# Hybrid network on one core: the first image's front and the mask's sorting issued in turns, scans started from their first 128 channels

## Chip, cores and metric

One core of a Trainium2 chip runs the whole program. The metric is the time of one execution on the device in microseconds (us). Its engines are called PE (TensorE, matrix multiplies), DVE (VectorE), ACT (ScalarE), POOL (GpSimd) and SP (SyncE, which here only issues DMAs).

## What is computed

The input is four images of 32 x 32 positions and 256 channels, so 1024 tokens per image. Cut to what matters here:

```python
# layer 0: state-space layer with a convolution
x = layernorm(src); x = x @ w_in + b_in                # 256 -> 512 channels
x = gelu(depthwise_conv3x3(x))                         # "front"
dt = softplus(proj_dt(x)); Bm, Cm = proj_bc(x)         # 64 states
h = exp(dt * A) * h + (dt * x) * Bm;  y = (h * Cm).sum(state)   # scan over 1024 tokens
out = src + layernorm(y + x * D_skip) @ w_out
# layer 1: grouped 3x3 convolution block
# layer 2: attention under a mask, then a mixture of 8 experts
mask = zeros(1024, 1024).at[edges[0], edges[1]].set(True)       # from a list of 69632 edges
# layer 3: state-space layer with 16 states, then a mixture of 8 experts
```

Each scan is linear in the tokens and independent for each pair of channel and state, so 512 channels x 64 states (layer 0) or 512 x 16 (layer 3) rows are scanned along 1024 tokens.

## The kernel before, in words

**Set-up.** `load_vectors` and `prepare` load vectors and weights, build the tables for the scans and store some prepared weights in DRAM. They run before everything else, and a scheduler of the framework orders their instructions.

**Stages.** The work of an image is cut into Python generators: `front(b)` (layer 0 up to the scan's operands), `middle(b)` (the end of layer 0, layers 1 and 2, layer 3 up to its scan's operands), `last(b)` (the end of layer 3 and its experts). Each `yield` is a tick. The table `STAGES` gives their order and the scan that each waits for; `advance` issues the next tick of the current stage. At the end of a front stands `steps`: for d in 0 to 3 (a d is 128 channels) and two halves of the tokens it projects dt on PE, takes the softplus on ACT, DVE and POOL, splits dt * x into three bf16 parts, and stores `dt` and `parts` in DRAM. These eight items go through five steps in a software pipeline (`project, add, split, low, store`); when both halves of a d are stored, `("parts", scan, d)` is put into `self.ready`. The last step of the middle stage is the same `steps` for layer 3.

**Scans.** `scans` runs the eight scans of `SCANS` in one chain of units: a unit is 128 rows of (channel, state), that is 64 units for each d of layer 0 and 16 for each d of layer 3, 1280 in all. For a unit, SP loads dt spread over the states (`load`, four units ahead), ACT takes the exponent (`decay`), PE spreads the parts over the states (`first`), DVE multiplies by B and scans, POOL multiplies by C, PE adds up the states (`pair`). `chunk`, called twelve units ahead (`AHEAD`), loads the rows of B and C at the start of a scan and the tile `S` of parts at the start of each d. Before a scan begins, `need` issues ticks of stages until all of that scan's parts are in `self.ready`.

**Who goes when.** In the scanning part the order of the instructions is the order in which Python issues them (`tc.manual_schedule`). Between the units, up to two ticks of stages are issued where a clock kept by `Metered` says that the other engines have time. All of these instructions are recorded with line L120 in the profile.

**The beginning.** `run` issues `front(0)` and `mask_prepare` to the end, outside of the manual order, in pools of their own; the framework's scheduler mixes them. Only then are the pools of the scans opened.

```python
            for _ in self.front(0):
                pass
            self.mask_prepare()
```

**The mask.** `mask_prepare` fills the mask in DRAM (4 MB) with a large negative number, loads the edges, turns them with PE, computes for each edge its place in the mask or none, and sorts the 544 values of each partition on DVE, in 68 rounds of `max` and `match_replace` (L980, L981), so that the edges in use stand in front. The places go to the tile `where` (L986). `scatter` writes zeros to those places, one indirect DMA of 128 words per column of `where`, from POOL's queue; 64 are always issued, later columns only where some partition has so many. One piece of it is issued per unit of the first scan. In the end POOL's queue copies the mask, cast to bf16.

Of the kernel before, what the change touches and what calls it, by code (L numbers as in the profile page):

```python
# [7 lines left out]
F32 = mybir.dt.float32  # L8
# [5 lines left out]
PSUM = bass.MemoryType.PSUM  # L14
DRAM = bass.MemoryType.DRAM

P = 128
# [5 lines left out]
DC = DI // P  # L23
# [7 lines left out]
SCANS = ((0, 0), (0, 1), (3, 0), (0, 2), (3, 1), (0, 3), (3, 2), (3, 3))  # L31

STAGES = (
    ("front", 1, None), ("front", 2, None), ("front", 3, None), ("middle", 0, (0, 0)),
    ("middle", 1, (0, 1)), ("middle", 2, (0, 2)), ("middle", 3, (0, 3)), ("last", 0, (3, 0)),
    ("last", 1, (3, 1)), ("last", 2, (3, 2)),
)
SAFE = 40.0
AHEAD = 12


# [83 lines left out]
class Hybrid:  # L125
# [213 lines left out]
    def scans(self, mp, psum):  # L339
# [7 lines left out]
        nc = self.nc  # L347
# [11 lines left out]
        def chunk(k):  # L359

            if k >= len(units):
                return
            scan, d, c, i, j = units[k]
            if (c, i, j) != (0, 0, 0):
                return
            n = self.states[scan[0]]
            if d == 0:
                self.need(scan)
                bct = self.mem["bc", *scan]
                pair = []  # L370
                for t in range(2):
                    x = mp.tile([P, L], F32, tag=f"rows{t}", name=f"rows{t}", bufs=2)
                    for g in range(P // n):
                        nc.sync.dma_start(x[g * n : (g + 1) * n, :], bct[t * n : (t + 1) * n, :])
                    pair.append(x)
                rows[scan] = pair
            S = mp.tile([3 * 32, 4, L], BF16, tag="S", name="S", bufs=2)
            for s in range(3):
                nc.sync.dma_start(
                    S[32 * s : 32 * s + 32, :, :],  # L380
                    self.mem["parts", *scan, d][s].rearrange("(j p) t -> p j t", p=32),
                )
            chunks[scan, d] = S
# [67 lines left out]

        for k in range(AHEAD):
            chunk(k)
# [5 lines left out]
        for k in range(len(units) + 4):  # L459
# [4 lines left out]
            if k < len(units):  # L464
                a, inp = state.pop(k)
# [9 lines left out]
                pair(k - 2)  # L475
            yield

    def need(self, scan):

        late = False  # L480
        while ("parts", *scan, DC - 1) not in self.ready:
            if self.advance() is None:
                raise RuntimeError(f"{scan} waits for a stage that waits for it")
            late = True
        if late:

            self.clock.update(dict.fromkeys(self.clock, max(self.clock.values())))
# [15 lines left out]
    def run(self):  # L503

        self.done, self.ready = set(), set()
        self.todo, self.stage = list(STAGES), None
        nc, tc = self.nc, self.tc
        with tc.tile_pool(name="fps", bufs=1, space=PSUM) as pp:
            self.side_psum(pp)
            for _ in self.front(0):  # L510
                pass
            self.mask_prepare()
        with tc.tile_pool(name="scan", bufs=1) as mp, tc.tile_pool(
            name="scps", bufs=1, space=PSUM
        ) as psum, tc.tile_pool(name="sdps", bufs=1, space=PSUM) as side, tc.manual_schedule():
            self.side_psum(side)
            scatter = self.scatter()
            clock = self.clock = dict.fromkeys(Metered.COST, 0.0)
            self.nc = Metered(nc, clock)
            for n, _ in enumerate(self.scans(mp, psum)):  # L520
                if n % 2:
                    next(scatter, None)
                now = clock["vector"]
                for e in clock:
                    clock[e] = max(clock[e], now - LAG)
                for _ in range(TICKS):
                    if max(clock.values()) > clock["vector"] + LEAD or self.advance() is None:
                        break
            while self.advance() is not None:
                pass  # L530
            self.nc = nc
        assert not self.todo
        with tc.tile_pool(name="lps", bufs=2, space=PSUM) as pp:
            self.side_psum(pp)
            for _ in self.last(NB - 1):
                pass
# [371 lines left out]
    def mask_prepare(self):  # L908
# [5 lines left out]
        nc, tc = self.nc, self.tc  # L914
# [7 lines left out]
        nc.vector.memset(self.zero, 0.0)  # L922
        self.where = self.const.tile([P, ne], I32, name="where")
        self.more = self.const.tile([1, len(SCATTERS)], I32, name="morei")
        with tc.tile_pool(name="mprep", bufs=1) as mp, tc.tile_pool(
            name="mps", bufs=2, space=PSUM
        ) as pm:
            neg = mp.tile([P, 2048], F32, name="neg")
            nc.gpsimd.memset(neg, NEG)
            flat = self.mask.rearrange("(q p f) o -> q p (f o)", q=4, p=P)  # L930
            for q in range(4):
                nc.sync.dma_start(flat[q], neg)

            ends = mp.tile([P, 2, ne], F32, name="ends")
            for a in range(2):
                raw = mp.tile([P, full + 1, P], I32, tag="raw", name="raw", bufs=2)
                nc.sync.dma_start(
                    raw[:, :full, :],
                    edges[a, : full * P * P].rearrange("(q r p) -> r q p", r=P, p=P),
                )  # L940
                nc.sync.dma_start(
                    raw[:rest, full, :], edges[a, full * P * P :].rearrange("(r p) -> r p", p=P)
                )
                rawf = mp.tile([P, full + 1, P], F32, tag="rawf", name="rawf", bufs=2)
                nc.vector.tensor_copy(rawf[:, :full, :], raw[:, :full, :])
                nc.vector.tensor_copy(rawf[:rest, full, :], raw[:rest, full, :])
                for q in range(full + 1):
                    m = P if q < full else rest
                    ps = pm.tile([P, P], F32, tag="e", name="ps_e")
                    nc.tensor.transpose(ps[:, :m], rawf[:m, q, :], self.ident[:m, :m])  # L950
                    nc.vector.tensor_copy(ends[:, a, q * P : q * P + m], ps[:, :m])
            wrap = mp.tile([P, 2, ne], F32, name="wrap")
            nc.vector.tensor_scalar(wrap, ends, 0.0, float(L), ALU.is_lt, ALU.mult)
            nc.vector.tensor_tensor(ends, ends, wrap, ALU.add)

            ok = mp.tile([P, 2, ne], F32, name="ok")
            nc.vector.tensor_scalar(ok, ends, 0.0, None, ALU.is_ge)
            nc.vector.tensor_scalar(wrap, ends, float(L), None, ALU.is_lt)
            nc.vector.tensor_tensor(ok, ok, wrap, ALU.mult)
            nc.vector.tensor_tensor(ok[:, 0, :], ok[:, 0, :], ok[:, 1, :], ALU.mult)  # L960
            nc.vector.tensor_scalar(ends, ends, 0.0, float(L), ALU.max, ALU.min)

            lin = mp.tile([P, ne], F32, name="lin")
            nc.vector.scalar_tensor_tensor(
                lin, ends[:, 1, :], float(L), ends[:, 0, :], ALU.mult, ALU.add
            )
            nc.vector.scalar_tensor_tensor(lin, lin, 1.0, ok[:, 0, :], ALU.add, ALU.mult)
            cnt = mp.tile([P, 1], F32, name="cnt")
            nc.vector.tensor_reduce(cnt, ok[:, 0, :], AX.X, ALU.add)
            ps = pm.tile([P, P], F32, tag="e", name="ps_c")  # L970
            nc.tensor.transpose(ps[:1, :], cnt, self.ident)
            top = mp.tile([1, 1], F32, name="top")
            nc.vector.tensor_reduce(top, ps[:1, :], AX.X, ALU.max)
            more = mp.tile([1, len(SCATTERS)], F32, name="more")
            for i, (first, _) in enumerate(SCATTERS):
                nc.vector.tensor_scalar(more[:, i : i + 1], top, float(first), None, ALU.is_gt)
            nc.vector.tensor_copy(self.more, more)
            order = mp.tile([P, ne], F32, name="sorted")
            for r in range(0, ne, 8):
                nc.vector.max(out=order[:, r : r + 8], in_=lin)  # L980
                nc.vector.match_replace(  # L981
                    out=lin, in_to_replace=order[:, r : r + 8], in_values=lin, imm_value=0.0
                )
            nc.vector.tensor_scalar(lin, order, 0.0, 2.0 * L * L, ALU.is_le, ALU.mult)
            nc.vector.scalar_tensor_tensor(lin, order, -1.0, lin, ALU.add, ALU.add)
            nc.vector.tensor_copy(self.where, lin)  # L986

    def scatter(self):

# [129 lines left out]
    def shift(self, fp, qT, kT, mT):  # L1119
# [28 lines left out]

        nc.vector.tensor_scalar(most[:, 0:1], most[:, 0:1], SAFE * SAFE, None, ALU.is_lt)
        nc.vector.tensor_scalar(most[:, 0:1], most[:, 0:1], -1.0, 1.0, ALU.mult, ALU.add)  # L1150
# [579 lines left out]
```

## Time and profile before

| | us |
|---|---|
| Median of 3 runs | 7051.57 (7046.13 to 7058.23) |
| Profiled execution, own time | 7061.6 |
| Span of its instructions | 7059.5 |
| Granted PE clock, mean | 0.81 |

| Stretch of the profiled execution | from | to |
|---|---|---|
| Front 0: norm, convolutions, projections | 37.6 | 144 |
| Front 0: `steps`, until its last store is issued | 141 | 209 |
| Rounds of the sort | 171 | 301 |
| Scan (0, 0) | 317.7 | 1386.5 |
| Scans (0, 1), (3, 0), (0, 2), (3, 1), (0, 3) | 1387.8 | 5464.4 |
| Scan (3, 2) | 5465.7 | 6327.7 |
| Scan (3, 3) | 6329.1 | 6643.6 |
| Rest, with `last(3)` | 6643.6 | 7059.5 |

The page of the profile names an engine, a line of the program and an operation as `output<-inputs`. Its slices cut the span in 40 equal parts of 176.5 us; each digit is the share in tenths that an engine was busy. A line of waits gives who waited, for whom, the sum, how often, and the longest, in us. A line of a timeline gives start and duration in us, engine, line, operation, and in brackets how long the engine had been idle and what ended that. An indirect DMA's row on POOL is the time that POOL worked on it, and its landing is a separate number.

### The profile page before, as it was taken

The page shows a single profiled execution, that of the slowest core. Times are in us where ns is not written, and L with a number is a line of the kernel's source. Part 1 is how long each engine was busy: PE and PEld are TensorE (multiplying, and loading weights), DVE is VectorE, ACT ScalarE, POOL GpSimd, SP SyncE. Part 2 cuts the span into 40 slices and gives each one's busy share as a digit, 9 for nine tenths or more (in the row PEclk, how much of TensorE's full clock was granted, in tenths as well). Part 3 has the DMA queues.
Part 4 walks back from the last instruction along what each step waited for, and adds up shares of the span by engine and source line. Part 5 has one row for each costly group of instructions (what it writes and reads, how often), then busy time and mean ns, then how long its engine had stood idle before and what let it go on. Part 6 is the DMA issues. An engine that isn't in the chain of part 4 may idle for free. (4 is left out here: it accounts for less than half of the span.)

```text
span 7059.5 us, 66331 instructions
## 1 busy us (share of the span) xinstructions
PE 5383.6 (76%) x20516; PEld 2218.2 (31%) x20516; DVE 5212.0 (74%) x4477; ACT 3462.1 (49%) x4162; POOL 3650.0 (52%) x1801
## 2 busy tenths in 40 slices
PE   7185876578898567879779668898698677957979
PEld 3020221032253022224235332242254322513556
DVE  2787898887898986789889877898899831247511
ACT  3254666244477324447658434577386332244511
POOL 1288677664556754555766554556656520045300
PEclk9585876578888567979879778898698889877989
DMA  2355666654456565446656654456666620135421
GB/s 82 77 139 158 161 178 167 169 143 120 115 143 176 160 172 136 119 116 171 176 151 164 178 144 120 115 143 178 165 168 165 162 70 6 44 107 152 113 63 33
DMA packets 395053, 939.03 MB, mean 133 GB/s; under 512 B 83268, under 2 KB 165776, under 8 KB 393040
## 3 DMA queue, kind: packets, MB, share of 16 engines
q1 hardware_dynamic: 392512, 932.10, 49.0%
q8 instruction: 172, 2.82, 0.2%
q0 software_dynamic: 2128, 2.13, 0.2%
q14 instruction: 241, 1.97, 0.1%
HBM read 844.17 MB, written 93.95 MB: 133 GB/s over the span
## 5 line engine op out<-in xcount | busy, mean ns | idle before, releaser
L120 POOL TENSOR_TENSOR h<-h,rows 128x1024 f32<-128x1024 f32 x1280 | 3024.2, 2365 | 2138.8 <-DVE h L120 1756.0
L120 DVE TENSOR_TENSOR_SCAN h<-dA,ps_rep 128x1024 f32<-128x1024 f32 x1280 | 2924.7, 2285 | 228.0 <-issue 94.6
L120 DVE TENSOR_TENSOR ps_rep<-ps_rep,rows 128x1024 f32<-128x1024 f32 x1280 | 1553.0, 1213 | 338.7 <-PE ps_rep L120 317.0
L120 ACT ACTIVATE dA<-dA,A_L_conv_A_log 128x1024 f32<-128x1024 f32 x1024 | 1152.8, 1145 | 695.2 <-DMA dA<-dt 600.6
L120 PE MATMUL ps_rep<-S,spread_L_conv_A_log 96*128 96x512 bf16 x2048 | 763.2, 463 | 899.6 <-DVE h L120 731.7
L120 PE MATMUL ps_y<-h,collect_L_conv_A_log 128*32 128x512 f32 x4096 | 750.2, 755 | 91.1 <-POOL h L120 91.1
L120 ACT ACT_TABLE_LOAD x494 | 633.8, 1283 | 174.7 <-DMA dA<-dt 115.0
L120 PEld LDWEIGHTS <-spread_L_conv_A_log 96*128 96x128 bf16 x2048 | 164.5, 103 | 1661.3 <-DVE h L120 1213.5
L120 PE MATMUL ps_h<-xTm,we 128*128 128x512 f32 x1280 | 605.2, 609 | 7.6 <-ACT h_m L120 6.6
L120 PE MATMUL ps_e<-we,h_m 128*128 128x256 f32 x2560 | 587.9, 381 | 10.1 <-ACT h_m L120 10.1
L120 ACT ACTIVATE p<-ps_sc 128x512 f32<-128x512 f32 x512 | 277.9, 595 | 587.2 <-PE ps_sc L120 573.8
L120 ACT ACTIVATE dA<-dA,A_L_attn_A_log 128x1024 f32<-128x1024 f32 x256 | 293.6, 1148 | 490.1 <-DMA dA<-dt 456.4
L120 PEld LDWEIGHTS ps_e<-we,h_m 128*128 128x128 f32 x2560 | 481.8, 190 | 140.6 <-issue 46.0
L120 PE MATMUL ps_at<-p,v 128*32 128x512 f32 x1024 | 363.6, 627 | 63.1 <-ACT p L120 55.7
L120 PE MATMUL ps_rep<-S,spread_L_attn_A_log 96*128 96x512 bf16 x512 | 191.4, 464 | 280.8 <-DVE h L120 239.2
L120 ACT ACTIVATE h_m<-ps_h,cols 128x512 f32<-128x512 f32 x320 | 216.5, 687 | 302.2 <-PE ps_h L120 299.3
L120 DVE SCALAR_TENSOR_TENSOR tb<-ps_e,cw,tb 128x256 f32<-128x256 f32 x448 | 192.6, 473 | 200.5 <-PE ps_e L120 200.5
L120 PEld LDWEIGHTS ps_h<-xTm,we 128*128 128x128 f32 x1280 | 242.4, 193 | 288.1 <-issue 236.3
L120 PE MATMUL ps_sc<-qT,kT 32*128 32x512 f32 x1024 | 300.7, 663 | 0.0
L120 PE MATMUL ps_at<-p,ones 128*32 128x512 f32 x1024 | 280.1, 627 | 0.0
L120 DVE RECIPROCAL sums<-sums 128x512 f32<-128x512 f32 x16 | 53.6, 3353 | 253.4 <-ACT sums L120 253.4
L120 PEld LDWEIGHTS ps_y<-h,collect_L_conv_A_log 128*32 128x32 f32 x4096 | 98.8, 119 | 450.4 <-issue 234.3
(406 smaller groups left out, 5703.5 us busy)
## 6 DMA issues: line engine op xcount, KB each, us to landing
dA<-dt SPq DMA_DIRECT2D x2048, 256.0 KB
dA<-dt SPq DMA_DIRECT2D x2048, 64.0 KB
we<-in_L_ffn_W_dram SPq DMA_DIRECT2D x64, 512.0 KB
parts<-parts SPq DMA_DIRECT2D x64, 384.0 KB
S<-parts SPq DMA_DIRECT2D x96, 256.0 KB
dt<-sp_r SPq DMA_DIRECT2D x64, 256.0 KB
y<-yo SPq DMA_DIRECT2D x128, 128.0 KB
y_back<-y SPq DMA_DIRECT2D x64, 256.0 KB
```

The lines of the kernel that those rows point to most:

```text
L120: return got(*args, **kw)
```

## The change

Front 0 becomes the first entry of `STAGES`, so it is issued by `need` and `advance` in the manual order, like the other fronts. `mask_prepare` becomes a generator, and `scatter` is its end. While `need` issues ticks, it issues two pieces of the mask's work (`SORTS`) after each tick; between the units of the scans one piece follows every unit, as the scatters did before. The first piece loads the edges, six empty pieces follow, then come the turned edges, then the 68 rounds one per piece. The fill of the mask is issued after the edges' loads and turns instead of ahead of the loads. The transposes of the mask take their PSUM tiles from the pool of the stages. `need` asks for the parts of one d instead of all four, and `chunk` calls it for every d. The memory of the sort and that of the scans are then held at the same time.

```diff
 STAGES = (
-    ("front", 1, None), ("front", 2, None), ("front", 3, None), ("middle", 0, (0, 0)),
+    ("front", 0, None), ("front", 1, None), ("front", 2, None), ("front", 3, None), ("middle", 0, (0, 0)),
...
+SORTS = 2
...
             n = self.states[scan[0]]
+            self.need(scan, d)
             if d == 0:
-                self.need(scan)
...
-    def need(self, scan):
+    def need(self, scan, d):
 
         late = False
-        while ("parts", *scan, DC - 1) not in self.ready:
+        while ("parts", *scan, d) not in self.ready:
             if self.advance() is None:
                 raise RuntimeError(f"{scan} waits for a stage that waits for it")
             late = True
+            for _ in range(SORTS):
+                next(self.mask_work, None)
...
-        with tc.tile_pool(name="fps", bufs=1, space=PSUM) as pp:
-            self.side_psum(pp)
-            for _ in self.front(0):
-                pass
-            self.mask_prepare()
...
-            scatter = self.scatter()
+            self.mask_work = self.mask_prepare()
...
                 if n % 2:
-                    next(scatter, None)
+                    next(self.mask_work, None)
...
-        with tc.tile_pool(name="mprep", bufs=1) as mp, tc.tile_pool(
-            name="mps", bufs=2, space=PSUM
-        ) as pm:
+        with tc.tile_pool(name="mprep", bufs=1) as mp:
             neg = mp.tile([P, 2048], F32, name="neg")
             nc.gpsimd.memset(neg, NEG)
-            flat = self.mask.rearrange("(q p f) o -> q p (f o)", q=4, p=P)
-            for q in range(4):
-                nc.sync.dma_start(flat[q], neg)
...
+                raws.append(raw)
+            yield from [None] * 6
+            for a, raw in enumerate(raws):
                 rawf = mp.tile([P, full + 1, P], F32, tag="rawf", name="rawf", bufs=2)
                 nc.vector.tensor_copy(rawf[:, :full, :], raw[:, :full, :])
                 nc.vector.tensor_copy(rawf[:rest, full, :], raw[:rest, full, :])
+                yield
                 for q in range(full + 1):
                     m = P if q < full else rest
-                    ps = pm.tile([P, P], F32, tag="e", name="ps_e")
+                    ps = self.ps("ps_e", (P, P))
                     nc.tensor.transpose(ps[:, :m], rawf[:m, q, :], self.ident[:m, :m])
                     nc.vector.tensor_copy(ends[:, a, q * P : q * P + m], ps[:, :m])
+                yield
+            flat = self.mask.rearrange("(q p f) o -> q p (f o)", q=4, p=P)
+            for q in range(4):
+                nc.sync.dma_start(flat[q], neg)
...
-            ps = pm.tile([P, P], F32, tag="e", name="ps_c")
+            ps = self.ps("ps_c", (P, P))
...
                     out=lin, in_to_replace=order[:, r : r + 8], in_values=lin, imm_value=0.0
                 )
+                yield
...
             nc.vector.tensor_copy(self.where, lin)
+        yield from self.scatter()
```

More of the change, by code (lines that the diff above doesn't have):

```diff
@@ L924, in mask_prepare @@
         self.more = self.const.tile([1, len(SCATTERS)], I32, name="morei")
-        with tc.tile_pool(name="mprep", bufs=1) as mp, tc.tile_pool(
-            name="mps", bufs=2, space=PSUM
-        ) as pm:
+        with tc.tile_pool(name="mprep", bufs=1) as mp:
             neg = mp.tile([P, 2048], F32, name="neg")
             nc.gpsimd.memset(neg, NEG)
-            flat = self.mask.rearrange("(q p f) o -> q p (f o)", q=4, p=P)
-            for q in range(4):
-                nc.sync.dma_start(flat[q], neg)
             ends = mp.tile([P, 2, ne], F32, name="ends")
+            raws = []
             for a in range(2):
```

## Prediction

> **What bounds the kernel now.** I read the page's slices first, then the busy time by stretches, then the waits of SP's queue, then the timelines at the two places where the slices show VectorE (DVE) idle or alone.
>
> ```profile
> PE   7185876578898567879779668898698677957979
> DVE  2787898887898986789889877898899831247511
> ```
>
> Each digit is 176.5 us. From slice 3 to 31 DVE is 80 to 90% busy: the eight scans (1280 units, of one 2285 ns scan and one 1213 ns multiply each: a unit costs 3.5 us of DVE) set the pace, and all other stages run beside them. Two places are outside this pace: the first two slices, before the scans run, and slices 33 to 36, where DVE falls to 1 to 4 while PE works.
>
> The first place, by stretches (us, then busy us and count of PE, PEld, DVE, ACT, POOL):
>
> ```profile
> 100.00:120.00 20.00, 20.00 (x48) 8.74 (x47) 0.00 (x0) 3.44 (x5) 0.00 (x0) 1.00 0.07 27
> 200.00:220.00 20.00, 0.00 (x0) 0.00 (x0) 16.42 (x33) 2.07 (x4) 6.06 (x5) 0.50 0.18 61
> 260.00:280.00 20.00, 0.00 (x0) 0.00 (x0) 19.13 (x39) 0.00 (x0) 0.00 (x0) 0.50 0.00 0
> ```
>
> While PE runs the front's convolutions DVE does nothing; later DVE sorts while nobody else works. The waits of SP's queue say who is kept waiting:
>
> ```profile
> SPq L374 <- DVE where L986: 92.7, 1, 92.7
> ```
>
> The first loads of the scan (L374) wait 92.7 us for the sort's last output, because the scan pools take the sort's memory. The front's last store was issued at 209.3; the loads go at 302.4, and the first scan starts at 317.7: 15.3 us from loads to scan.
>
> The second place is the last scan, (3, 3). Its `need` is called twelve units early, and in program order everything of the middle of image 3 then stands before unit 1204. DVE's scans stop from 5743 to 6280. The end of that stop:
>
> ```profile
> 6246.61 0.68 DVE L120 SCALAR_TENSOR_TENSOR sp_e<-ps_dt,sp_e 128x512 f32<-128x512 f32 x1
> 6252.25 0.80 DVE L120 TENSOR_TENSOR sp_x<-sp_l,parts 128x512 f32<-128x512 f32 x1 [4.96 <-ACT parts L120]
> 6252.98 0.68 DVE L120 SCALAR_TENSOR_TENSOR sp_e<-ps_dt,sp_e 128x512 f32<-128x512 f32 x1
> ...
> 6278.38 1.22 DVE L120 TENSOR_TENSOR ps_rep<-ps_rep,rows 128x1024 f32<-128x1024 f32 x1
> ```
>
> An item of `steps` takes 6.35 us, and the scan resumes at 6278.4, after the eighth.
>
> **What the Trainium skill says.** "DMA: Bandwidth & Descriptors", section "Anatomy of one DMA — SWDGE (gpsimd) path": a DMA issued from GpSimd has a fixed part of about 2.0 us, most of it the write's receipt from memory. The trace agrees: the 64 scatters of 128 words land 2.1 us after issue at the least, 3.2 in the median, 8.2 at the most. Its section "Latency and other measured facts" says that a lighter HBM load makes that part smaller; before, every scatter ran beside the scan's loads (148 GB/s), so I take the low end where nothing else moves. "SBUF — State Buffer", section "Who interferes with whom": a DVE instruction with two SBUF inputs contends with a GpSimd one that reads SBUF. The trace agrees: a 128x1088 tensor_tensor took 1.29 us with POOL idle (L954), 2.23 with it busy (L959). I use the short ones, since POOL is idle where they go.
>
> **The change, part by part.** Times are those of the profiled execution (span 7059.5, own time 7061.6); the median of the runs, 7051.6, is 10.0 below the latter, and I take the difference over to it.
>
> (a) *Front 0 now issues in program order behind w_x and w_dt.* w_x waited until 34.1 for the store of w2 (2.5 us in SP's waits); x went ahead of it at 31.0. Now x goes at 35 and lands at about 42 (before: 37.4). Edge loads go before the 4 MB mask fill: about 2.4 MB at 215 GB/s from 34 on, so at 47 (before: 50.8).
>
> (b) *Sorting stands in front of the norm on DVE.* `need` draws two pieces per front tick; the order of the changed program has three stats, then the transposed ends, the mask's arithmetic and eight of 68 rounds before the norm's `ln_v`, and two more rounds before `ln_b`. From 47: two casts, 0.63 us each pair, with five copies through PE, 2.6: 6.5 for both; five stats between and behind them, 1.05 each: 5.3; the arithmetic at the uncontended rows: 9.9; ten rounds of 1.58 (MAX8 0.73, load 0.09, replace 0.71, gaps): 15.8; the norm's chain over ACT: 2.8 + 0.2. `ln_b` ends at 87.6 instead of 44.2. The front's matmuls, 96 us of nearly gapless PE, start **43 us late**.
>
> (c) *The other 58 rounds* run on DVE beside the convolutions, which need no DVE: 58 x 1.58 + 1.7 = 93.6, so `where` is there at 181. The front's steps begin on PE at 140.9 + 43 = 184. So the sort is hidden, at the cost of (b).
>
> (d) *Scatters stand in front of the steps on POOL.* By the changed program's order 30 of the 64 scatters come before the first `sp_l`, two more at each tick, 40 in all before the first scan's POOL multiply. Each waits for the landing of the one before (POOL rows: 23 waits, 30.3 us). Period: landing 2.15 + 0.3 from landing to next issue (as at 413.2: landed 5.4, next 5.7 later) = 2.45. Bounds: 1.2 (only POOL's 1.0 and a gap, if they overlap) and 3.5 (median landing + 0.3). From 181.4 the 30 take 72 us, to 253.5, while ACT, DVE and PE wait behind POOL. Then POOL's own list until the dt store that stands before the scan's loads on SP: four groups of adds less one multiply, 15, two `low` 2.3, three pairs of scatters 3.5 each: about 28. Loads at 281.7; 15.3 later less one ACT table load, 1.3, which the steps' exponent has made needless: first scan at **296** against 317.7. **Gain 22** (bounds from the period: +59 and -9).
>
> (e) *Remaining steps of front 0 run inside the scan*, items 4 to 7: by the fronts 2 and 3, each costs the scan 34 us over 64 units (units of 3.55), most of it in eight items, so 13 to 17 here. But units 0 to 87 took 403 us, 57 more than those 34 and pure pace explain: scatters, the four switches behind them, and start. With 24 scatters instead of 64 left I take half back, 28. **Gain about 10**, between -15 and +30. From unit 224 to 1152 the changed DVE order is the old one, so nothing else moves.
>
> (f) *The last scan begins after two of eight items.* The fifth item's `sp_e` is at 6253.0: scan resumes 24.7 earlier. Three `sp_e` and three `sp_x`, some 4.5 us, and waits for POOL in order (about 4 us per item in the scan, by front 3) come back inside it; SP, which spends 3.7 us per unit on issues here, waits with its stores too. **Gain 11**, between 0 and 22. Earlier scans of images 1 to 3 had their parts hundreds of us early: nothing there.
>
> Sum: 22 + 10 + 11 = 43. 7051.6 - 43 = **7008**.
>
> **Rivals.** *Scatters overlap.* If a scatter costs POOL only 1.2 us, (d) gains 59 and the sum is 80: 6972. For it: POOL is busy 1.0 of each; against it: 23 waits in the trace name the previous landing. *Scatters land as before the change.* Period 3.5: start at 326, (d) costs 9, sum +12: 7040, hardly told from no change. For it: the median; against it: nothing else is moving then. *Slower: the scatter chain becomes the bound of the start.* Each of 30 scatters delays all four engines; the gains of (e) and (f) are used up, and the kernel is slower, from a period of 3.9 us on; at 4.6 (half way between median and the 5 to 8 us seen beside bursts) the scan starts at 359 and the kernel takes 7072. Against it: the bursts came from the scan's loads, which have not begun. *The change doesn't do what it says*: if the sort's memory still held the scan's loads, start would be bound by `where` at 181 only; the order shows no such delay, so it gives the same as the main case.
>
> **How the numbers follow.** About 0.2% (14 us) is what a measurement of this kernel can tell from no change. Main case 0.68, its own range 6982 to 7034 (the ends of (d) for periods of 2.1 and 2.9, and half of those of (e) and (f)); overlap 0.13; median landing 0.13, half of it faster by over 0.2%; slower chain 0.06. Faster 0.87, same 0.07, slower 0.06. Range 6960 to 7040: a tenth is left out at the low end, a tenth above.
>
> **What would show it.** Sort beside PE at 90 to 181, `ln_b` near 88; a POOL row of 30 scatters with landings of 2.1 to 2.3 and nothing else in 181 to 254; first scan near 296; units 0 to 87 in about 390; the stop's end about 25 us nearer to the eighth item. Wrong if the scatters' period is under 2 or over 3, or if the scan (0, 0) takes over 1085 or under 1040 us (before: 1068.8).

## The result, and the profile after

The changed kernel takes 6999.3 us in the median of 4 runs (6990.2 to 7000.6), the kernel before 7051.1 (7046.1 to 7058.2): a ratio of 0.9923, 95% interval 0.9906 to 0.994, so 52 us less. The profiled executions differ by 61.0 (7061.6 and 7000.6, spans 7059.5 and 6998.6), because that of before lay 10.5 above its median and that of after only 1.3. The spans divide like this:

| | before | after | difference |
|---|---|---|---|
| First scan begins | 317.7 | 279.9 | -37.8 |
| Scan (0, 0) | 1068.8 | 1071.6 | +2.8 |
| Next five scans, until (3, 2) begins | 4079.2 | 4079.0 | -0.2 |
| Scans (3, 2) and (3, 3) | 1177.9 | 1152.0 | -25.9 |
| Rest | 415.9 | 416.1 | +0.2 |

The page's slices (one digit is 175 us): DVE's first digit rises from 2 to 7, since the sort now runs in the first slice, beside PE; the hole in slices 33 to 36 has the same shape as before.

```profile
PE   6267877578898557879779778898698677867979
DVE  7379899887898986789889877898899830247511
```

The stretches that answer to those of before (us, then busy us and count of PE, PEld, DVE, ACT, POOL, then PE clock, DMA share, GB/s):

```profile
100.00:120.00 20.00, 20.00 (x48) 8.88 (x47) 19.14 (x39) 6.12 (x15) 0.00 (x0) 1.00 0.12 50
...
200.00:220.00 20.00, 0.00 (x0) 0.00 (x0) 0.00 (x0) 0.00 (x0) 7.91 (x9) 0.50 0.01 1
260.00:280.00 20.00, 3.60 (x6) 0.93 (x6) 2.67 (x4) 10.75 (x15) 12.80 (x11) 0.50 0.79 182
```

Between 100 and 120 PE and DVE are now both full. Between 200 and 220 PE, DVE and ACT do nothing, and POOL works 7.9 of 20 us, on nine instructions. Its timeline says which:

```profile
166.62 1.20 POOL L121 DMA_INDIRECT mask_dram<-zero,where  x1 [156.42 <-DVE where L121]
169.25 0.98 POOL L121 DMA_INDIRECT mask_dram<-zero,where  x1 [1.43 <-DMA mask_dram<-zero,where]
...
236.65 0.97 POOL L121 DMA_INDIRECT mask_dram<-zero,where  x1 [1.43 <-DMA mask_dram<-zero,where]
237.64 1.27 POOL L121 TENSOR_TENSOR sp_l<-sp_l,sp_e 128x512 f32<-128x512 f32 x1
```

Thirty scatters, the bracket of each naming the landing of the one before: 0.97 of work and 1.43 of waiting, a period of 2.40, from 166.6 to 237.6. They are 71 us in which the first item of `steps` waits behind them on POOL. In SP's queue, where the long wait ahead of the scan's first loads used to name the sort's last output, it now names POOL:

```profile
SPq L575 <- POOL sp_r L121: 83.3, 5, 69.8
```

(L575 stores dt, and the scan's first loads stand behind it; 69.8 of the 83.3 is one wait.) At the second place, DVE's timeline of the kernel before where the last scan resumes, first item and scan:

```profile
6227.86 0.69 DVE L120 SCALAR_TENSOR_TENSOR sp_e<-ps_dt,sp_e 128x512 f32<-128x512 f32 x1 [77.26 <-ACT sp_l L120]
...
6279.63 2.29 DVE L120 TENSOR_TENSOR_SCAN h<-dA,ps_rep 128x1024 f32<-128x1024 f32 x1
```

and of the changed kernel:

```profile
6191.11 0.69 DVE L121 SCALAR_TENSOR_TENSOR sp_e<-ps_dt,sp_e 128x512 f32<-128x512 f32 x1 [77.28 <-ACT sp_l L121]
...
6216.22 0.68 DVE L121 SCALAR_TENSOR_TENSOR sp_e<-ps_dt,sp_e 128x512 f32<-128x512 f32 x1
6216.82 1.22 DVE L121 TENSOR_TENSOR ps_rep<-ps_rep,rows 128x1024 f32<-128x1024 f32 x1
6222.89 0.69 DVE L121 TENSOR_TENSOR sp_x<-sp_l,parts 128x512 f32<-128x512 f32 x1 [4.86 <-ACT parts L121]
6223.50 0.69 DVE L121 SCALAR_TENSOR_TENSOR sp_e<-ps_dt,sp_e 128x512 f32<-128x512 f32 x1
6224.10 2.28 DVE L121 TENSOR_TENSOR_SCAN h<-dA,ps_rep 128x1024 f32<-128x1024 f32 x1
```

The scan's multiply stands behind the fifth item's `sp_e` instead of the eighth item's `sp_x`, and its scan behind the sixth's. From the first item's `sp_e` to that scan it is 33.0 us instead of 51.8, and to the multiply 25.7 instead of 50.5.

### The profile page after: what moved, and what is told of

It is laid out like the page before. It is cut to its first block, busy times and chain, and to the rows that moved or that the text cites. A ratio compares the mean times of both kernels' runs of the same rounds, so it can differ in the third digit from the quotient of the medians.

```text
span 6998.6 us, 66229 instructions
## 1 busy us (share of the span) xinstructions
PE 5362.1 (77%) x20433; PEld 2215.4 (32%) x20516; DVE 5202.2 (74%) x4476; ACT 3455.6 (49%) x4157; POOL 3646.1 (52%) x1801
## 5 line engine op out<-in xcount | busy, mean ns | idle before, releaser
L121 ACT ACTIVATE dA<-dA,A_L_conv_A_log 128x1024 f32<-128x1024 f32 x1024 | 1152.0, 1145 | 714.8 <-DMA dA<-dt 629.4
L121 DVE SCALAR_TENSOR_TENSOR tb<-ps_e,cw,tb 128x256 f32<-128x256 f32 x448 | 192.7, 473 | 200.4 <-PE ps_e L121 200.4
L121 PE MATMUL ps_cv<-pad,diag 128*128 128x512 f32 x576 | 260.0, 593 | 0.0
```

Source lines behind the costliest of these rows:

```text
L121: return got(*args, **kw)
```

## Experiments

Each kernel was timed beside the kernel before on the same chip; the ratio is to that. The starts, the durations of scans and the waits are from the profiled execution of each. One yardstick for them: the kernel before and the one called `falone` have the same program up to the last scan, and their scans (0, 0) took 1068.8 and 1059.6 (the five scans behind it 4079.2 and 4072.9). Differences of 9 us in a single profile of that scan therefore prove nothing. The start has a spread of its own, of up to 5 us, told under (a) below.

| kernel | ratio to before (95%) | first scan at | scan (0, 0) | (3, 2) + (3, 3) |
|---|---|---|---|---|
| changed | 0.9923 (0.9906 to 0.994) | 279.9 | 1071.6 | 1150.7 |
| late | 0.9828 (0.9814 to 0.9841) | 217.5 | 1066.1 | 1152.0 |
| whole | 0.9988 (0.9979 to 0.9996) | 327.1 | 1041.4 | 1173.3 |
| falone | 0.9967 (0.9955 to 0.9979) | 317.8 | 1059.6 | 1154.0 |
| noscat | 0.9792 (0.9776 to 0.9808) | 217.9 | 1044.6 | 1152.6 |
| norm_first | 0.9879 (0.9864 to 0.9894) | 241.0 | 1083.3 | 1149.2 |
| late_norm | 0.9817 (0.9803 to 0.983) | 205.1 | 1067.6 | 1150.4 |
| late_mid | 0.9798 (0.9785 to 0.9812) | 192.7 | 1066.4 | 1151.9 |
| gap | 0.994 (0.9926 to 0.9953) | 283.0 | 1075.9 | 1152.4 |
| spread | 0.9907 (0.9893 to 0.992) | 280.1 | 1055.7 | 1148.7 |
| late_mid_spread | 0.9782 (0.9769 to 0.9795) | 195.7 | 1061.1 | 1150.7 |

### late: the scatters stay in the scan

```diff
             for _ in range(SORTS):
-                next(self.mask_work, None)
+                if not self.sorted:
+                    next(self.mask_work, None)
```

(`sorted` is set ahead of `yield from self.scatter()`.)

> The changed kernel, but `need` draws no more of the mask's work once the sort is done, so one scatter stands before the first `sp_l` instead of 30, and 63 of 64 are issued one per unit of the scan. Theory (the chained scatters are the bound of the start): the first scan starts about 71 us earlier (29 scatters of 2.40) and up to 10 more for the scatters that stood between the first `sp_l` and the loads, so at 195 to 209 instead of 279.9; 40 more scatters inside scan (0, 0) cost it up to 15; in all about 65 to 70 faster than the changed kernel, 6930 to 6940. Rival A (each scatter holds up the scan's POOL by its 2.4 us as it did the start): scan (0, 0) grows by 60 to 90 and nothing is won, about 7000. Rival B (something else, such as PE's late convolutions, holds the start): the start moves by less than 30, 6970 or more.

Measured: 6925.3 (before: 7049.4), a further 1% below the changed kernel and 5 below the theory's range. The first scan began 62.4 earlier, at 217.5, later than the theory's 195 to 209, and scan (0, 0) was no longer, with 63 scatters in it instead of 26. The chained scatters were the bound of the start. The start moved less than the 71 because something else was close behind. POOL's timeline, and DVE's:

```profile
171.68 1.20 POOL L121 DMA_INDIRECT mask_dram<-zero,where  x1 [161.47 <-DVE where L121]
181.48 1.26 POOL L121 TENSOR_TENSOR sp_l<-sp_l,sp_e 128x512 f32<-128x512 f32 x1 [8.61 <-DVE sp_e L121]
```

```profile
180.70 0.69 DVE L121 SCALAR_TENSOR_TENSOR sp_e<-ps_dt,sp_e 128x512 f32<-128x512 f32 x1 [9.33 <-ACT sp_l L121]
```

DVE ended the sort and then waited 9.3 for ACT, which waited for PE's late convolutions: here the front's delay by the sort is on the path, which the scatters had covered in the changed kernel. (The whole front also lay 5 us later in this execution, its first round of the sort at 58.3 instead of 53.2, for the reason told under (a) below. Counted from the first scatter, the first scan came 67.5 earlier.)

### whole: `need` waits for all four d again

```diff
-            self.need(scan, d)
+            self.need(scan, DC - 1)
```

> The changed kernel, but `need` waits for all four d as before the change. Four items and 14 scatters more stand before the first scan. Theory: it starts 45 to 58 us later (14 scatters of 2.40 and four items of about 6), near 330; scan (0, 0) is 25 to 36 shorter, because the late items and the handover from front 0 to front 1 are no longer inside it; scans (3, 2) and (3, 3) together take about 25 longer. Sum 7035 to 7050. Rival (the first scan gains nothing from its early start, what is left inside costs as much as it saves): start later by 50, (0, 0) shorter by 50, only the 25 of the last scans remain, 7025. Rival by the prediction's own sizes (late items cost 13 to 17, the last scan 11): 7050 or more, with (3, 2) and (3, 3) only 11 longer.

Measured: 7037.4, inside the range of the theory, and 0.12% below before. The first scan began 47.2 later than in the changed kernel, (0, 0) was 30.2 shorter, (3, 2) and (3, 3) together 22.6 longer. So the early start of the first scan is worth 17 net (47 won, 30 paid inside the scan), and that of the last scan 23. The turns alone, without the part per d, keep almost nothing of the gain, since 51 scatters then stand before the first scan.

### falone: the part per d alone, on the kernel before

```diff
-            if d == 0:
-                self.need(scan)
+            self.need(scan, d)
+            if d == 0:
                 bct = self.mem["bc", *scan]
```

(and `need` asks for `("parts", *scan, d)`.)

> The kernel before, with one part of the change alone: `need` asks for one d at a time. Front 0 and the sort stay ahead of the scans, so only scan (3, 3) can begin earlier. Theory (its early start is worth nearly the whole 24.7 us that the resume moves, since little comes back): 7025 to 7028, all of it in scans (3, 2) and (3, 3). Rival as predicted (half comes back inside the scan): 7040. Rival (the 25 us in the changed kernel come from its other parts): 7051.

Measured: 7024.8, 24.6 below before; (3, 2) and (3, 3) took 1154.0 together against 1176.4 before. The theory holds: the last scan's early start brings nearly all of the 24.7 by which its resume was to move, not 11.

### noscat: what the scatters cost inside the scan

```diff
-            nc.gpsimd.memset(neg, NEG)
+            nc.gpsimd.memset(neg, 0.0)
...
                 for j in range(first, end):
-                    zeros(j)
                     yield
```

> The changed kernel with the 64 scatters left out and the mask filled with 0, so all pairs of tokens are attended; the four switches and the cast of the mask stay. Theory: the first scan starts at 180 to 200, and scan (0, 0) keeps most of its excess over 256 units of 3.55 us (909), since that sits in the late items and the handover to front 1: 1045 to 1065. Total 6895 to 6920. Rival (the prediction's step (e): the scatters and what waits behind them cause half of the early units' excess): scan (0, 0) at 1035 or less, and units 0 to 87 in 375 or less.

Measured: 6901.9. The first scan begins at 217.9, as in `late`, later than expected, for it waits for the same convolutions. Scan (0, 0) at 1044.6 lies at the edge of the theory's range. Against `late`, which has 63 scatters in the scan and starts at the same time, (0, 0) is 21.5 shorter and the median 23.4 lower: some 0.34 us for a scatter inside the scan, against 2.40 for one in front of it. That is an estimate, because the two also differ in where front 1 begins (its x is loaded at unit 12 here, at unit 68 in `late`) and where the switches stand; for the same reason units 0 to 87 were no measure (383.2 here, 370.0 in `late`). `late` alone gives a bound: its units 0 to 63 hold 62 scatters, neither switches nor front 1's norm, and took 257.3, which is 33.3 more than 64 units of 3.5, so a scatter there cost 0.54 at the most. What remained inside `noscat` showed in POOL's timeline, where one of the scan's multiplies should follow the other by 3.6:

```profile
334.11 2.35 POOL L121 TENSOR_TENSOR h<-h,rows 128x1024 f32<-128x1024 f32 x1 [5.07 <-PE ps_cv L121]
340.34 2.36 POOL L121 TENSOR_TENSOR h<-h,rows 128x1024 f32<-128x1024 f32 x1 [3.87 <-issue]
347.06 2.34 POOL L121 TENSOR_TENSOR h<-h,rows 128x1024 f32<-128x1024 f32 x1 [4.36 <-issue]
353.64 2.35 POOL L121 TENSOR_TENSOR h<-h,rows 128x1024 f32<-128x1024 f32 x1 [4.24 <-issue]
```

"Issue" is time in which POOL waited for nothing that the profile shows. In program order the four switches behind the scatters stand here, one per unit: each reads a count into a register and branches, and takes some 4 us of POOL that count as idle. With units at 6.2 to 6.7 instead of 3.6, PE waited 5.7 us for POOL's `h` ahead of its `ps_y` matmuls, and behind these in PE's order stood the `ps_rep` matmuls for which DVE then waited 8.6 us.

### norm_first: the norm ahead of the sort

```diff
-            yield from [None] * 6
+            yield from [None] * 24
```

> The changed kernel with 24 empty pieces instead of six ahead of the turned edges, so that the norm's `ln_b` stands before the mask's arithmetic and all rounds on DVE; two scatters per tick as in the changed kernel, of which 12 instead of 30 then stand before the first `sp_l`. Theory (DVE's rounds without a gap set `where`, not the front): `ln_b` ends at 45, PE's convolutions end about 28 earlier, `where` stays within 6 of 167, the first scan starts at 236 to 244 (18 scatters of 2.40 fewer), and scan (0, 0) is up to 15 longer with 18 more scatters in it: 6960 to 6975. Rival (the sort only changes places with the front and `where` comes 28 later): first scan at 262 to 270, 6985 to 6995. Rival (the front's delay was itself on the path): the first scan also gains those 28, at 210 to 215, 6935.

Measured: 6968.8 (before: 7053.1). `ln_b` stood at 46.1 instead of 72.6, the last round began at 167.5 instead of 163.0, the first scan at 241.0: the theory in each. The start gained 38.9; since the sort ended 4.5 later here, that is 43.4 counted from the first scatter, which is what 18 scatters fewer make (43.2), and nothing beyond, although the front was 27 earlier: in the changed kernel the front's delay lay under the sort and the scatters. Scan (0, 0) was 12 longer; 18 more scatters lie in it (some 6 at 0.34 each), and POOL's switches and the load of x for front 1 (a wait of 19.8 in DVE's waits) fell together. How the 12 divide was not measured.

### late_norm: both

> The changed kernel with both edits: no scatters drawn by `need`, and the norm ahead of the mask's arithmetic. With the scatters gone from the start, the first `sp_e` stood 9.3 after `where` and waited for ACT, behind PE's late convolutions. Theory: the front is now early, the rounds are the bound, and only those 9 are won: `where` at about 168, first `sp_e` right behind it, first scan at 206 to 210, 6912 to 6920. Rival (the front's 28 us are won in full): first scan at 190, 6898. Rival (rounds end later, since they begin later): no gain, 6925 or more.

The edits are those of `late` and `norm_first`. Measured: 6923.6, above the theory's 6920, ratio 0.9817 against 0.9828 for `late`, with intervals that overlap: the total can't tell them apart. The profile can, at the place: `where` and the first `sp_e` on DVE's timeline, with no wait between them, and the first scan at 205.1. Of the 12.4 by which it came earlier, 9.3 are that wait; the rest is within what the set-up took less in this execution (x's load at 29.6 instead of 34.4, see (a)).

```profile
167.10 0.45 DVE L121 CAST where<-lin 128x544 int32<-128x544 f32 x1
167.46 0.69 DVE L121 SCALAR_TENSOR_TENSOR sp_e<-ps_dt,sp_e 128x512 f32<-128x512 f32 x1
```

The bound of the start is now DVE with its rounds; PE waits for it (15.7 us ahead of a pair of `ps_dt` matmuls, whose releaser is that `sp_e`).

### late_mid: the last rounds between the items

```diff
+            yield from [None] * 20
             for r in range(0, ne, 8):
                 nc.vector.max(out=order[:, r : r + 8], in_=lin)
```

(on top of `late_norm`)

> As the kernel with late scatters and the norm first, with 20 more empty pieces ahead of the rounds, so that the last ten rounds stand between the items of `steps` on DVE (two of 1.58 in each gap of about 5) instead of ahead of the first. Theory (the rounds ahead of `sp_e` were the bound): first `sp_e` at about 150, first scan at 185 to 192, 6893 to 6902. Rival (the rounds between the items lengthen each item by their 3.2): first scan at 200 or later, 6910 or more.

Measured: 6910.8, first scan at 192.7. The start is just beyond the theory's range; the total is above it and at the rival's, but it fell by 12.8 against `late_norm`, as much as the start (12.4): I had put the total of the step before too low. On DVE's timeline an item still takes 6.35, and its gap shrank from 4.96 to 1.92, filled by two rounds:

```profile
161.14 0.69 DVE L121 TENSOR_TENSOR sp_x<-sp_l,parts 128x512 f32<-128x512 f32 x1 [1.69 <-ACT parts L121]
161.75 0.68 DVE L121 SCALAR_TENSOR_TENSOR sp_e<-ps_dt,sp_e 128x512 f32<-128x512 f32 x1
...
167.39 0.80 DVE L121 TENSOR_TENSOR sp_x<-sp_l,parts 128x512 f32<-128x512 f32 x1 [1.92 <-ACT parts L121]
```

So the rounds between cost nothing, which the rival had denied. The first `sp_e` was at 155.7, not 150: it waited 2.0 for ACT, so front and sort are both at the bound there.

### gap: ticks between x's load and its stats

```diff
-                yield 1.0
+                for _ in range(1 if b == 0 else 12):
+                    yield 1.0
                 xT = fp.tile([P, 2, L], F32, name="xT0")
```

> The changed kernel with 12 ticks instead of one between the loads of fronts 1 to 3 and their first stats, so that the stats of the norm do not stand on DVE ahead of x's landing. Theory (of scan (0, 0)'s missing gain of 10, the handover from front 0 to front 1 is a part: x is loaded only once the last parts have landed, and DVE waits 15.8 for it): that wait goes, scan (0, 0) is 12 to 16 shorter, in all 6983 to 6990. Rival (the work that was behind the wait is late then and stops DVE elsewhere): no change, 6995 to 7003.

DVE's waits of the changed kernel from 280 to 690 (sum, how often, longest) hold the wait that this was to remove, the second line; the first is for `spread`, below:

```profile
DVE sp_x L121 <- ACT parts L121: 16.8, 3, 11.0
DVE ln_st L121 <- DMA x<-in_x_dram: 15.8, 1, 15.8
```

Measured: 7007.1, no gain (4 above the rival's range, with an interval that overlaps that of the changed kernel), and (0, 0) at 1075.9: the rival holds. The wait for x fell from 15.8 to 1.9, but beside it, on DVE's timeline, two waits for decays came:

```profile
448.34 2.29 DVE L121 TENSOR_TENSOR_SCAN h<-dA,ps_rep 128x1024 f32<-128x1024 f32 x1 [3.75 <-ACT dA L121]
...
458.94 2.29 DVE L121 TENSOR_TENSOR_SCAN h<-dA,ps_rep 128x1024 f32<-128x1024 f32 x1 [4.64 <-ACT dA L121]
```

That is 8.4 of the 13.9. Those decays waited for their loads (18.3 and 9.0 on ACT, each named `dA<-dt`). SP's queue tells why: x's load was issued at 448.1, having waited for the last parts to land in the memory that it reuses, and the scan's next loads stand behind it, at 449.1. The scan's own loads are as late as x, and taking one of the two waits away left the other.

### spread: the four switches apart

```diff
             self.clock.update(clock)
-            yield
+            yield from [None] * 8
```

> The changed kernel with the four switches behind the scatters eight units apart instead of one per unit. In the changed kernel POOL stands still for about 5 us at each of them, and DVE has an 11 us stop there in scan (0, 0). Theory (four in four units exceed POOL's 1.2 us of slack per unit; this, which the prediction did not price, is a part of the gain that scan (0, 0) is missing): that stop goes, (0, 0) is 10 to 14 shorter, 6984 to 6991. Rival (a switch costs the scan the same wherever it stands): no change, 6995 to 7003. Rival (the items of front 0 that stood there were the stop): no change either, and DVE's 11 us wait for `parts` stays.

Measured: 6986.1 (before: 7057.1), inside the range; the ratio's interval overlaps that of the changed kernel, so again the place decides. Its waits of DVE, from 280 to 680:

```profile
DVE ln_st L121 <- DMA x<-in_x_dram: 6.9, 1, 6.9
DVE sp_x L121 <- ACT parts L121: 6.2, 3, 3.0
```

The wait of 11.0 for `parts` (whose ACT waited for POOL) is gone, and that for x, which is loaded only when the last parts have landed, fell by 9 without being touched. Scan (0, 0) was 15.9 shorter, a little more than the 10 to 14 expected. The rival that blamed the items of front 0 is out, since its wait went while the items stayed.

### late_mid_spread: the version that the runs point to

> The kernel with late scatters, the norm first and the last rounds between the items, with the four switches eight units apart too: the version that the runs point to. Theory: 6 to 14 faster than without (6911), 6897 to 6905. Rival (here the switches' stop is already hidden, since front 1's items stand elsewhere): 6907 to 6914.

The edits are those of `late_mid` and `spread`. Measured: 6903.6 in the median (before: 7057.1), ratio 0.9782 (0.9769 to 0.9795): 2.2% faster than the kernel before, and 1.4% below the changed one by the ratio of the two ratios. Against `late_mid` the intervals overlap; that the switches' distance helps here is likely (units 64 to 71 took 43.2 instead of 50.6) but not shown.

## Why the prediction was right, step by step

The time, 7008, missed by 9, inside the range, in the likeliest case. The total hides one right chain and several errors of size that cancel. The mechanisms of (a) to (d) were the predicted ones; what happens inside the scans, (e) and the give-back of (f), was not.

**(a) x and the edges: mechanism right, and 5 us of luck.** x's load was put at 35, behind w_x, which waits for the store of w2 to land. SP's timeline of the changed kernel, and of `late`:

```profile
25.35 0.33 SPq L826 DMA_DIRECT2D w<-w  x1
...
29.30 0.42 SPq L645 DMA_DIRECT2D x<-in_x_dram  x1
```

```profile
30.49 0.33 SPq L828 DMA_DIRECT2D w<-w  x1
...
34.45 0.42 SPq L647 DMA_DIRECT2D x<-in_x_dram  x1
```

x goes 3.95 behind that store in both, and within 0.02 of that in all ten kernels with the change. But the store itself went at 25.4 to 25.7 in five of these kernels, at 27.4 to 27.8 in three, and at 30.5 in `late` and `noscat`, as in the kernel before (30.6). In these two x went at 34.5, where the prediction had 35. So the change alone does not bring the store forward. None of the edits touches the set-up, and the order of SP's issues and of PE's matmuls up to the store is the one of the kernel before in all of them; PE did the matmuls ahead of it faster in some of the profiled executions. The stretch from 22 to 24, changed kernel and `late`:

```profile
22.00:24.00 2.00, 2.00 (x8) 1.04 (x7) 1.61 (x4) 0.00 (x0) 0.00 (x0) 1.00 0.28 113
```

```profile
22.00:24.00 2.00, 2.00 (x5) 1.12 (x4) 0.53 (x1) 0.00 (x0) 0.00 (x0) 1.00 0.00 0
```

Eight matmuls started against five, while the clock on record reads 1.00 in both; why is open. In the changed kernel the first stats ran at 35.8 (42 predicted), and the first edges were there at 38.2 (47 predicted); some 5 of each is this luck, which was there in the profiled execution and is not shown for the others.

**(b) The sort ahead of the norm: mechanism right, size off.** DVE's timeline:

```profile
53.21 0.71 DVE L982 MAX8 sorted<-lin 128x8 f32<-128x544 f32 x1
...
66.94 0.16 DVE L121 TENSOR_SCALAR ln_v<-ln_mv 128x8 f32<-128x8 f32 x1
...
72.63 0.16 DVE L121 SCALAR_TENSOR_TENSOR ln_b<-ln_mv,ln_r 128x8 f32<-128x8 f32 x1
```

The order is the predicted one, eight rounds before `ln_v` and two before `ln_b`, but it ended at 72.8, not 87.6: 8.8 of the 14.8 are the edges of (a), 5 of them luck, and most of the rest are the stats, at 0.55 (0.4 and 0.18, partly overlapped) instead of 1.05, and the turning of the ends. Arithmetic (9.6 against 9.9) and rounds (1.58) were right. The front was 28 late, not 43. That it costs nothing by itself in the changed kernel was shown by `norm_first`, and that it costs where the scatters are gone, by `late`.

**(c) Rounds hidden beside PE: right.** The stretch from 100 to 120 shows it; `where` came at 166.6 instead of 181, by (a) and (b) alone.

**(d) The scatters: right.** Period 2.40 (predicted 2.45), 30 of them, nothing else running. From `where` to the first scan it took 113.3; the prediction had 114.6. The first scan came at 279.9 instead of 296 only because the chain began earlier. Of the gain of 37.8 at the start, 22 were predicted and 15 are (a) and (b). The rival in which they overlap is excluded by the period, the one with the chain as the bound for the worse (3.9 and more) by the landings, 2.1 to 2.4 while nothing else moved. The 26 issued after the scan began landed after 3.3 in the median, and the two issued at 271.8 and 280.4, beside the scan's first loads (DMA share 0.79 from 260 to 280), after 8.3 and 7.6: the bursts that this rival needed go with the scan's loads.

**(e) Late items inside the scan: the gain was not there.** A gain of 10 was put here; (0, 0) took 2.8 more than in the kernel before and 12 more than in `falone`, whose order there is the old one, and units 0 to 87 took 399.7, not 390. The step that failed is "I take half back, 28": the excess of the early units was put down to the number of scatters. By the estimate of `noscat` and `late`, 0.34 for a scatter inside the scan, 38 fewer there are worth 13, and by the bound of 0.54 at most 21. What did not go away are the four switches. They moved onto the units where the last items of front 0 and the handover to front 1 now lie (x of front 1 is loaded only once the last parts have landed), and cost some 16 in the profile of `spread`, 13 in its median. The late items' price, 13 to 17, can't be separated from the handover: `whole` pays 30 less in (0, 0) without either and with 13 scatters fewer, some 4 of it by the price above. How much of the rest is the handover stays open, since `gap` only traded its wait for others.

**(f) The last scan: mechanism right, give-back wrong.** Counted from the first item, the multiply came 24.8 earlier, as predicted, and the scan behind it, which the next item's `sp_x` and `sp_e` precede in program order, 18.8 earlier. By the end of (3, 3) the gain was 26, not 11; `falone` shows it alone, with 22 there and 24.6 in the total. Half was to be lost to `sp_e` and `sp_x` inside the scan and to SP. But the 17 units from that scan on took 69.3 with the items between them, against 67.9 without: 1.4 was lost there. The kernel before shows why they cost so little, in SP's queue and on DVE just after the resume:

```profile
6289.77 23.37 SPq L394 DMA_DIRECT2D dA<-dt  x48
```

```profile
6297.56 2.29 DVE L120 TENSOR_TENSOR_SCAN h<-dA,ps_rep 128x1024 f32<-128x1024 f32 x1 [4.08 <-ACT dA L120]
```

A unit of layer 3 needs eight such loads, so SP takes 3.9 us per unit (23.37 / 48 x 8), more than DVE's 3.5; the 17 units took 4.0 each (67.9 / 17). In these units SP sets the pace, and DVE waits for it anyway. In the changed kernel the extra DVE instructions fill those waits, SP's loads begin earlier, and the later wait for loads, at unit 1222, is 16.75 instead of 21.75. That this is the reason is read from the traces; no run takes SP's pace away.

So the sum was right partly by luck: the start brought 16 more than predicted (some 5 of it an early set-up), (e) 13 less, (f) 15 more, in profiled executions that lie 9 further apart than the medians. The working has slips that move little: 58 x 1.58 + 1.7 is 93.3, not 93.6; 28 less 13 to 17 is 11 to 15, put at 10; and DVE's slices 3 to 31 read 6 to 9, not 8 to 9 throughout.

## What to carry to other kernels

In this kernel a chain of DMAs that wait for each other cost its whole latency where nothing ran beside it, 2.40 us each, and by estimate a seventh of that inside the scan: drawn into a stage with idle engines it looked like free work, but in program order it stood in front of the work on POOL for which all others waited. Look, for each thing that is interleaved, at what is queued behind it on its own engine, not at whether the machine is idle. And when a start is moved earlier, what the old delay covered (here the front behind the sort, and small fixed pieces such as switches) comes next; price where those pieces land, not only how many they are.

## What the runs showed of the hardware

A branch on POOL with a value read from SBUF took about 4 us of the engine, in time that no row shows (3.9 to 4.4 in the stretch of `noscat` above, where nothing else stands between the scan's multiplies). And a 128x512 subtraction on DVE took 2.16 us where POOL multiplied beside it, against 0.69 with POOL idle (the `sp_x` at 6222.89 above):

```profile
422.46 2.16 DVE L121 TENSOR_TENSOR sp_x<-sp_l,parts 128x512 f32<-128x512 f32 x1 [10.96 <-ACT parts L121]
```

This is the contention that the prediction quoted from the Trainium skill, "SBUF — State Buffer", section "Who interferes with whom"; in the kernel before (2.23 against 1.29) the factor was 1.7, here it is 3.1 (2.16 against 0.69).
